# A transformer block: the first batch's softmax sums moved from TensorE to GpSimd and VectorE, loads spread over two queues, and the quantized tiles moved from GpSimd's queue to ScalarE's and SyncE's

## The chip, the core and the metric

The kernel runs on one core of a Trainium2 chip. Its engines are TensorE (PE; PEld is its loading of weights), VectorE (DVE), ScalarE (ACT), GpSimd (POOL) and SyncE (SP), which only starts transfers here. All five run their own list of instructions in order and meet at semaphores. The metric is the device time of one execution in microseconds (us), compared by medians.

## The reference

The input `x` is 4 batches of 512 rows with 512 columns. The block is an attention with 16 heads of width 32 and one shared key and value head, followed by a gated feed-forward layer with weights rounded to -1, 0 and 1; both parts end in a residual sum and a layer norm:

```python
q = rotary(heads(x @ Wq + bq)); k = rotary(x @ Wk + bk); v = x @ Wv + bv
scores = q @ k.T / sqrt(32)
ctx = softmax(scores) @ v
x = layernorm(x + ctx @ Wo + bo)
quantize(w) = clip(round(w / (mean(abs(w)) + 1e-8)), -1, 1)      # w1, w2: 1408x512, w3: 512x1408
hidden = sigmoid(x @ quantize(w1).T) * (x @ quantize(w2).T)
x = layernorm(x + hidden @ quantize(w3).T)
```

All inputs and outputs are 32-bit floats. The softmax needs, for each row and head, the sum of 512 exponentials. Where and how these sums are made in batch 0 is the heart of the change.

## The kernel before, in words

**Steps.** The main loop (L855) runs over 64 steps: 4 batches `b`, in each 4 chunks `c` of four heads, in each 4 blocks `t` of 128 key rows. I number them 0 to 63; batch 0 is steps 0 to 15. A step calls `scores` (L404): eight passes of matmuls of `kT` by `q` and eight passes that subtract the row maxima (`negm`) into two PSUM tiles `ps`, then two exponentials `es` on ScalarE. A 32-bit matmul is two passes in the trace. Then `weigh` (L445) multiplies the exponentials of the step before by `v` into `acc`, and in batch 0 `count` (L454) multiplies them by a matrix of ones into `den`: the sums. In batches 1 to 3 `den` is not used. There GpSimd adds the four blocks' exponentials into `total` (L422 to L438), and VectorE adds up over the rows afterwards.

**Maxima ahead.** In the same step `find_maxima` (L812) works 7 steps ahead (`LEAD`): matmuls `pmax` into the same two PSUM tiles that `ps` used (pool `ps_sc`, two buffers), and VectorE's maxima `mx` over them. For the steps of batch 0 this is `row_maxima` (L360), with 32-row operands; for later batches `maximum` (L371), with 128-row operands `qr` loaded from memory.

**Filling.** Between these stand pieces of other work (`fill.draw`, L763): about 1.8 us of TensorE work a step in batch 0 (`pace`, L857), which are projections `pk` and `pq` of the next batches (`project_in`, L262) with their rotations on VectorE (`turn`, L238); later also the output projection `po` and the feed-forward layer `gu`. Small chains of work (`late`) are advanced by `due` (L792), twice a step; one call is a slot.

**After a chunk.** `normalize` (L461) begins three slots after the last step of a chunk. In batch 0 it copies `den` on ScalarE, sends it to memory (`sent`), loads it back with 128 partitions (`few`), takes the reciprocal on VectorE, sends that (`flat`), and loads it with each row spread over 32 partitions (`rden`). In later batches it reduces `total` with two VectorE instructions (`part`), sends the result, loads it with 32 partitions (`few`), and reduces, inverts and transposes it before `flat`. In the end GpSimd multiplies `ctxT` by `rden` (L516).

**Quantizing.** `quantized` (L158) is a list of 66 jobs of one 128x512 tile (256 KB): 33 to find the mean of absolute values (`junk`, ScalarE), and 33 that quantize (`sgn` on ScalarE, `raw` on VectorE) and store. Jobs 0 to 20 come ahead of step 0, three after each of 7 maxima; two jobs a step follow in batch 0; the rest in batch 1. So the first weight's tiles are quantized in jobs 22 to 32 and the second's from job 44. Job k first starts the load of job k+4. Tiles of even jobs have four buffers, of odd ones five, so the load for an even job reuses the buffer of the job eight before it: if that was a quantizing one, it has to be stored first. A store is issued two jobs after its tile was quantized (L216 to L219). Loads and stores both stand in GpSimd's list (L178, L218). `sgn` is in SBUF up to step 16 and in PSUM after that (L208 to L212).

**The beginning.** SyncE issues, in this order, two small bias loads, the key and value weights, four tiles of the transposed input (`load_xT`, L121), then the query weights, `cos`, `sin` and others (L129 to L144). TensorE meanwhile does 24 matmuls of ones that nobody uses (`WARM`, L53 and L152). The first real work is `pk`, on the key and value weights and the four tiles.

**Order.** `pin` keeps each engine's instructions in the order in which the program writes them (`InOrder`, L70); `mm`, `move` and `transpose` are helpers, so most instructions carry the lines L75, L80, L83 or L86. `move` puts a transfer in SyncE's list; a wait in that list holds all later ones.

## Time and profile before

| what | value |
|---|---|
| median of 3 runs | 671.13 us (670.32 to 673.02) |
| the profiled execution | 672.56 us |
| its span, first to last instruction | 670.8 us |
| step 0 of batch 0 begins its exponentials | 49.61 us |
| step 16 (batch 1) begins its exponentials | 164.36 us |
| `den` matmuls, all in batch 0 | 128 passes, busy 16.7 us in all |
| GpSimd's adds `total`, batches 1 to 3 | 144, busy 184.3 us |
| GpSimd's issues of `raw` loads and `w` stores | 66 and 33, 0.55 us each |
| VectorE's `part`, batches 1 to 3 | 24, mean 1.23 us |

The page lists each engine's busy time and the chain of work that ended last. The chain says which instruction's end each step was waiting for; an engine's busy time does not. Groups of instructions are named out<-in by the program's tiles, followed by shapes, the count, busy time, the mean of one in ns, and the idle time ahead of them with what ended it. The timeline lists instructions in order: start, duration, engine, line, operation, tiles. Matmul ends are modelled, and matmuls that work in different rows or columns of the array overlap: eight passes of `den`, nearly 0.6 us each, take under 1 us of the chain together.

### The profile page before, as it was taken

To read this page: it belongs to the slowest core of one execution; us is meant where nothing else is said; L and a number is where in the kernel's file an instruction comes from. 1 tells how busy PE (TensorE), PEld (TensorE's weight loads), DVE (VectorE), ACT (ScalarE), POOL (GpSimd) and SP (SyncE) were. 2 spreads that over 40 slices of the span, in tenths; PEclk is the share of its full clock that TensorE was granted. 3 is DMA by queue.
4 is the path that set the end of the run, shared out by engine and by line. 5 is a ranking of instruction groups with operands and counts; after the bars stand their busy time and mean duration, and the time that the engine had idled before them with its cause. 6 is when DMAs were issued, how large, how long until landed. Compare 5 with 4: busy or idle time off the path is not lost.

```text
span 670.8 us, 9406 instructions
## 1 busy us (share of the span) xinstructions
PE 644.7 (96%) x3222; PEld 358.5 (53%) x3222; DVE 430.0 (64%) x619; ACT 282.8 (42%) x441; POOL 324.4 (48%) x414
## 2 busy tenths in 40 slices
PE   9989999999999989999999899999999999999995
PEld 6333333443333355665456466654555685778884
DVE  1896766587787867766666966676635553464335
ACT  1466555655443644333334445233435421234213
POOL 0615334535987776376666375576574802202000
PEclk9999999999999999999999999999999999999998
DMA  8755668688575286355132456351232364236531
GB/s 283 248 192 175 205 199 261 186 286 276 162 245 172 92 259 202 116 169 162 54 84 82 125 164 215 124 172 29 73 100 67 126 217 148 79 109 213 183 107 63
DMA packets 60671, 107.78 MB, mean 161 GB/s; under 512 B 14592, under 2 KB 15360, under 8 KB 60624
## 3 DMA queue, kind: packets, MB, share of 16 engines
q1 hardware_dynamic: 52560, 81.10, 38.5%
q0 software_dynamic: 7920, 25.96, 11.8%
q8 instruction: 25, 0.41, 0.3%
q14 instruction: 22, 0.18, 0.1%
q10 hardware_dynamic: 144, 0.13, 0.1%
HBM read 84.06 MB, written 23.10 MB: 160 GB/s over the span
## 4 chain that ended last, share of the span: by engine, by line
PE 81%; DVE 9%; DMA 4%; ACT 3%; issue 2%; SPq 1%; POOL 0%; DVEq 0%; ACTq 0%; POOLq 0%
PE gu L80 23%; PE po L80 19%; PE ps L80 11%; PE pmax L80 8%; PE acc L80 7%; PE pq L80 7%; DVE mx L75 3%; PE den L80 2%; DMA wg<-w 2%; ACT es L75 2%; PE pk L80 1%; DVE xt L75 1%; PE warm L80 1%; SPq L83 1%; DMA xT<-in_xT 1%
## 5 line engine op out<-in xcount | busy, mean ns | idle before, releaser
L75 DVE TENSOR_REDUCE mx<-pmax 128x1 f32<-128x512 f32 (+1 forms) x159 | 158.1, 1007 | 81.3 <-PE pmax L80 81.1
L75 ACT ACTIVATE es<-ps 128x1024 f32<-128x1024 f32 x128 | 124.2, 1022 | 141.9 <-PE ps L80 133.9
L80 PE MATMUL gu<-y,wg 128*128 128x512 f32 x704 | 172.9, 395 | 2.0 <-DMA wg<-w 1.1
L80 PEld LDWEIGHTS gu<-y,wg 128*128 128x128 f32 x704 | 131.1, 188 | 38.4 <-issue 4.7
L75 POOL TENSOR_TENSOR total<-total,es 128x512 f32<-128x512 f32 x96 | 123.8, 1319 | 45.2 <-ACT es L75 45.1
L80 PE MATMUL po<-wd,h 128*128 128x512 f32 x352 | 87.0, 395 | 4.2 <-DVE y L75 2.9
L75 POOL TENSOR_TENSOR total<-es 128x512 f32<-128x512 f32 x48 | 60.5, 1290 | 55.8 <-ACT es L75 55.8
L80 PE MATMUL pmax<-kr,qr 128*128 128x512 f32 x192 | 75.2, 455 | 3.7 <-ACT es L75 2.2
L80 PEld LDWEIGHTS po<-wd,h 128*128 128x128 f32 x352 | 64.9, 188 | 22.5 <-DVE y L75 4.6
L75 ACT CAST h<-hw 128x512 fp32r<-128x512 f32 x44 | 27.3, 620 | 100.7 <-DVE hw L75 100.7
L80 PE MATMUL acc<-es,v 128*32 128x512 f32 x512 | 68.2, 605 | 0.0
L80 PEld LDWEIGHTS pmax<-kr,qr 128*128 128x128 f32 x192 | 33.6, 188 | 57.0 <-ACT es L75 20.9
L75 DVE SCALAR_TENSOR_TENSOR hw<-th,gu 128x512 f32<-128x512 f32 x44 | 30.2, 687 | 46.9 <-PE gu L80 46.8
L80 PE MATMUL po<-wo_sb,ctxT 128*128 128x512 f32 x128 | 58.9, 593 | 0.3 <-DVE hw L75 0.3
L80 PE MATMUL ps<-negm,ones_r 2*128 2x512 f32 x256 | 58.2, 788 | 0.0
L75 DVE SCALAR_TENSOR_TENSOR xt<-po,xt 128x512 f32<-128x512 f32 x48 | 32.8, 684 | 38.1 <-PE po L80 38.1
L75 DVE TENSOR_TENSOR h<-hw,h 128x512 fp32r<-128x512 f32 x44 | 42.1, 957 | 21.7 <-ACT h L75 21.4
L80 PE MATMUL ps<-qT,kT 32*128 32x512 f32 x384 | 55.6, 640 | 0.0
L75 POOL DMA_DIRECT2D raw<-in_wf x66 | 36.1, 549 | 37.4 <-DMA w<-raw 26.7
L80 PE MATMUL pq<-xT,wq_sb 128*128 128x512 f32 x112 | 53.0, 601 | 1.0 <-ACT v L75 1.0
L75 ACT ACTIVATE th<-gu 128x512 f32<-128x512 f32 x44 | 26.3, 598 | 49.1 <-PE gu L80 49.0
L80 PEld LDWEIGHTS po<-wo_sb,ctxT 128*128 128x128 f32 x128 | 24.1, 189 | 22.0 <-issue 19.2
(98 smaller groups left out, 639.2 us busy)
## 6 DMA issues: line engine op xcount, KB each, us to landing
wg<-w SPq DMA_DIRECT2D x88, 256.0 KB
raw<-in_wf POOLq DMA_DIRECT2D x66, 256.0 KB, 4.6
qr<-qp SPq DMA_DIRECT2D x96, 128.0 KB
wd<-w SPq DMA_DIRECT2D x44, 256.0 KB
w<-raw POOLq DMA_DIRECT2D x33, 256.0 KB, 4.9
qp<-q SPq DMA_DIRECT2D x48, 128.0 KB
rden<-flat SPq DMA_DIRECT2D x64, 64.0 KB
xt<-in_x SPq DMA_DIRECT2D x16, 256.0 KB
```

Source lines behind the costliest of these rows:

```text
L75: return lambda *args, **kw: pin(getattr(self.engine, name)(*args, **kw))
L80: pin(nc.tensor.matmul(out, lhsT=lhsT, rhs=rhs, start=start, stop=stop))
L83: pin(nc.sync.dma_start(out=out, in_=in_))
```

## The change

Five edits:

1. `WARM` is 10 instead of 24. The key and value weights are loaded first; the four input tiles are issued in turn by ScalarE's queue and SyncE's; the bias loads follow in ScalarE's queue. Later calls of `load_xT` use SyncE alone, as before.
2. `count` and its matmuls are gone. The adds of `total` on GpSimd are now made in batch 0 too.
3. `normalize` takes the way of batches 1 to 3 for batch 0 (the two `part` reductions without a slot between them there), and begins four slots after the chunk instead of three in batch 0.
4. The loads of the tiles to be quantized are issued by ScalarE.
5. The stores of the quantized tiles are issued by SyncE.

```diff
-    WARM = 24
+    WARM = 10
...
-    def load_xT(n):
+    def load_xT(n, engines=(nc.sync,)):
-        for _ in range(n):
+        for k in range(n):
...
-                move(batches[b].xT[c], xT[b, :, c, :])
+                pin(engines[k % len(engines)].dma_start(out=batches[b].xT[c], in_=xT[b, :, c, :]))
...
-    move(bkv_sb, bkv)
-    move(bq_sb, bq)
     move(wkv_sb, wkv)
-    load_xT(NC)
+    load_xT(NC, (nc.scalar, nc.sync))
+    pin(nc.scalar.dma_start(out=bkv_sb, in_=bkv))
+    pin(nc.scalar.dma_start(out=bq_sb, in_=bq))
     move(wq_sb[0], wq[:, 0])
...
-                pool.dma_start(out=raws[k], in_=wf[m, f])
+                pin(nc.scalar.dma_start(out=raws[k], in_=wf[m, f]))
...
-                    pool.dma_start(out=w.bitcast(F32), in_=q)
+                    move(w.bitcast(F32), q)
...
-        if b > 0:
-            if t == 0:
-                s.first = es
+        if t == 0:
+            s.first = es
...
-    def count(b, c, t, es):
-        s = batches[b]
-        if t == 0:
-            s.den = ps_acc.tile([P, T], F32, tag="den", name="den")
-        columns(s.den, ones[:, 0:HD], es, t == 0, t == NT - 1)
...
-                if j == 0 and c + 1 < NC:
-                    yield
+            if j == 0 and b > 0 and c + 1 < NC:
+                yield
...
-            sums = work.tile([P, T], F32, tag="sums", name="sums", bufs=1)
-            act.copy(sums, s.den)
-            yield
-            sent = dram.tile([NG, T], F32, tag="flat0", name="sent", bufs=3)
-            move(sent, sums.rearrange("(i r) k -> i r k", r=HD)[:, 0])
-            yield
-            few = small.tile([P, NG * T // P], F32, tag="few", name="few")
-            move(few, sent.rearrange("i (r j) -> (i r) j", r=HD))
...
-            dve.reciprocal(few, few)
-            move(flat.rearrange("i (r j) -> (i r) j", r=HD), few)
...
-        if last is not None and last[0] == 0:
-            count(*last)
...
-            begin = slot + 3
+            begin = slot + (4 if b == 0 else 3)
```

More of the change, by code (lines that the diff above doesn't have):

```diff
@@ L421, in scores @@
             es.append(e)
-        if b > 0:
-            if t == 0:
-                s.first = es
-            elif t == 1:
-                s.total = [work.tile([P, 2, T], F32, tag=f"total{j}", name="total", bufs=1) for j in range(2)]
-                for j in range(2):
-                    for i in range(2):
-                        pool.tensor_tensor(
-                            s.total[j][:, i, :], s.first[j][:, i, :], es[j][:, i, :], ALU.add
-                        )
-            else:
-                for j in range(2):
-                    for i in range(2):
-                        pool.tensor_tensor(
-                            s.total[j][:, i, :], s.total[j][:, i, :], es[j][:, i, :], ALU.add
-                        )
+        if t == 0:
+            s.first = es
+        elif t == 1:
+            s.total = [work.tile([P, 2, T], F32, tag=f"total{j}", name="total", bufs=1) for j in range(2)]
+            for j in range(2):
+                for i in range(2):
+                    pool.tensor_tensor(
+                        s.total[j][:, i, :], s.first[j][:, i, :], es[j][:, i, :], ALU.add
+                    )
+        else:
+            for j in range(2):
+                for i in range(2):
+                    pool.tensor_tensor(
+                        s.total[j][:, i, :], s.total[j][:, i, :], es[j][:, i, :], ALU.add
+                    )
         return es
@@ L464, in normalize @@
         flat = dram.tile([NG, T], F32, tag="flat1", name="flat", bufs=3)
-        if b > 0:
-            n = T // HD
-            part = work.tile([P, NG * n], F32, tag="sums", name="part", bufs=1)
-            for j in range(2):
-                dve.tensor_reduce(
-                    part[:, ts(j, 2 * n)],
-                    s.total[j].rearrange("p i (a r) -> p (i a) r", r=HD),
-                    AX.X, ALU.add, apply_transpose=True,
-                )
-                if j == 0 and c + 1 < NC:
-                    yield
-            yield
-            parts = dram.tile([P // HD, HD, NG * n], F32, tag="parts", name="parts", bufs=3)
-            move(parts.rearrange("o r k -> (o r) k"), part)
-            yield
-            few = work.tile([HD, P // HD + 2, NG * n], F32, tag="rot_b", name="few", bufs=1)
-            move(few[:, 0 : P // HD, :], parts.rearrange("o r k -> r o k"))
-            yield
-            if c + 1 < NC:
-                yield
-            whole, lines = few[:, P // HD, :], few[:, P // HD + 1, :]
-            dve.tensor_reduce(whole, few[:, 0 : P // HD, :].rearrange("r o k -> r k o"), AX.X, ALU.add)
-            dve.reciprocal(whole, whole)
-            dve.transpose(lines, whole)
-            move(
-                flat.rearrange("(b h) (a r) -> (h a) b r", b=2, r=HD),
-                lines.rearrange("x (b r) -> x b r", b=2),
-            )
-        else:
-            sums = work.tile([P, T], F32, tag="sums", name="sums", bufs=1)
-            act.copy(sums, s.den)
-            yield
-            sent = dram.tile([NG, T], F32, tag="flat0", name="sent", bufs=3)
-            move(sent, sums.rearrange("(i r) k -> i r k", r=HD)[:, 0])
-            yield
-            few = small.tile([P, NG * T // P], F32, tag="few", name="few")
-            move(few, sent.rearrange("i (r j) -> (i r) j", r=HD))
-            yield
-            if c + 1 < NC:
-                yield
-            dve.reciprocal(few, few)
-            move(flat.rearrange("i (r j) -> (i r) j", r=HD), few)
@@ new lines, in normalize @@
+        n = T // HD
+        part = work.tile([P, NG * n], F32, tag="sums", name="part", bufs=1)
+        for j in range(2):
+            dve.tensor_reduce(
+                part[:, ts(j, 2 * n)],
+                s.total[j].rearrange("p i (a r) -> p (i a) r", r=HD),
+                AX.X, ALU.add, apply_transpose=True,
+            )
+            if j == 0 and b > 0 and c + 1 < NC:
+                yield
+        yield
+        parts = dram.tile([P // HD, HD, NG * n], F32, tag="parts", name="parts", bufs=3)
@@ new lines, in normalize @@
+        move(parts.rearrange("o r k -> (o r) k"), part)
+        yield
+        few = work.tile([HD, P // HD + 2, NG * n], F32, tag="rot_b", name="few", bufs=1)
+        move(few[:, 0 : P // HD, :], parts.rearrange("o r k -> r o k"))
+        yield
+        if c + 1 < NC:
+            yield
+        whole, lines = few[:, P // HD, :], few[:, P // HD + 1, :]
+        dve.tensor_reduce(whole, few[:, 0 : P // HD, :].rearrange("r o k -> r k o"), AX.X, ALU.add)
+        dve.reciprocal(whole, whole)
+        dve.transpose(lines, whole)
@@ L509, in normalize @@
+        move(
+            flat.rearrange("(b h) (a r) -> (h a) b r", b=2, r=HD),
+            lines.rearrange("x (b r) -> x b r", b=2),
+        )
         yield
```

## The prediction

> **What bounds the kernel now.** I read the page's first part, then the chain of waits, then the timeline of one step, then busy time step by step. Times are from the profiled execution (672.56 us, span 670.8, so 1.8 outside the span).

> ```profile
> span 670.8 us, 9406 instructions
> PE 644.7 (96%) x3222; PEld 358.5 (53%) x3222; DVE 430.0 (64%) x619; ACT 282.8 (42%) x441; POOL 324.4 (48%) x414
> ```

> TensorE looks full everywhere, so a removed matmul seems worth its whole time. The chain of one step of batch 0 seems to agree:

> ```profile
> 100.95 1.91 PE pk L80 x4
> 102.86 1.87 PE ps L80 x12
> 104.73 0.99 PE acc L80 x8
> 105.72 0.86 PE den L80 x8
> 106.58 1.09 PE pmax L80 x8
> ```

> `den`, the matmuls that the change drops, has 0.86 us of a step of 6.73. But the timeline of that step shows what stands beside it:

> ```profile
> 104.56 1.94 ACT L75 ACTIVATE es<-ps 128x1024 f32<-128x1024 f32 x2 [3.05 <-PE ps L80]
> 106.51 1.16 PE L80 MATMUL pmax<-kT,room 32*128 32x512 f32 x8
> 107.69 2.36 DVE L75 TENSOR_REDUCE mx<-pmax 128x2 f32<-128x1024 f32 x2 [4.38 <-PE pmax L80]
> 110.10 0.19 PEld L80 LDWEIGHTS ps<-room,kT 32*128 32x128 f32 x2 [0.28 <-DVE mx L75]
> ```

> The two exponentials end at 106.50, and `pmax` starts at 106.51: its two PSUM tiles are those that the exponentials empty. So `acc` and `den` fill exactly the time of the exponentials. Two reductions `mx` follow `pmax` on VectorE, and the second half of the next `ps` waits for the second of them. The loop is thus ScalarE, TensorE, VectorE in turn, with TensorE's filling inside it.

> **The change part by part.**

> 1. *The beginning: 10 warm-up matmuls for 24, the loads on two queues.* The warm-up passes alone:

> ```profile
> 1.50:4.35 2.85, 2.85 (x13) 2.85 (x14) 0.20 (x1) 1.00 0.63 143
> 4.35:7.20 2.85, 2.85 (x15) 2.85 (x14) 0.00 (x0) 1.00 0.84 206
> 7.20:9.77 2.57, 2.57 (x24) 2.54 (x22) 0.00 (x0) 1.00 1.04 352
> ```

> Twenty-eight passes in the first 5.70 us are 0.204 us each, then 24 in 2.57 are 0.107 each: TensorE doubles its pace at 7.2, though the clock column (sixth; 1.00) shows nothing. Ten matmuls are 20 passes at 0.204, so they end at 1.5 + 4.1 = 5.6 instead of 9.9. `pk` then needs its five tiles, 1.31 MB. Stretches of 2.5 us up to 7.5 and one up to 9.77 moved 2, 186, 247 and 356 GB/s: 1.09 MB by 7.5, so 1.31 at about 8.1. The two small bias loads no longer stand ahead (SP's issue of `wkv_sb` comes at 1.64 after two others; the first was at 0.73), so about 7.2, when the last quarter of `pk` is wanted. If the doubling comes at 7.2 as before, `pk` (8 passes, 3.44 us on the chain) does 1.9 passes at half pace from 5.6, and 6.1 × 0.43 = 2.6 more: it ends at 9.8 or, with a little waiting for loads, 10.0, against 13.37. **Gain 3.4.** Bounds: 1.7 (`pk` at half pace for 3.4 us more) and 4.0. From 22 to 46 us the chain is mostly VectorE's `mx` and rotations, no load, so it shifts whole. After 12 us the changed startup loads are not near the path.

> [...]

> 2. *64 `den` matmuls (128 passes) gone.* What is gained is what the loop gains, not 16 × 0.86. In steps 1 to 8, `pmax` works in row groups: its first half can start when the first exponential ends, its second only after the second, as now. Its end stays; but the first `mx` starts some 0.9 earlier, and `ps` shrinks from up to 1.87 to 1.31 (the chain's undisturbed ones). I take 6.73 to 6.3: 0.4 a step. In steps 9 to 15 `pmax` is the full-width form, whose first half moves ahead too. There the trace has the very step, in batch 1, without `den` and with one filling of 1.9:

> ```profile
> 181.26 1.94 ACT L75 ACTIVATE es<-ps 128x1024 f32<-128x1024 f32 x2 [2.83 <-PE ps L80]
> 187.04 1.02 ACT L75 ACTIVATE es<-ps 128x1024 f32<-128x1024 f32 x1 [2.74 <-PE ps L80]
> ```

> 5.78 from step to step, against 6.32 to 6.71. So TensorE's and ScalarE's part allows 8 × 0.4 + 7 × 0.64 = **7.7**. ScalarE also loses four copies of 0.62, beside other work: nothing.

> 3. *Sums to GpSimd and VectorE.* GpSimd gets 12 adds for each of four chunks at 1.3, 62 us, and loses 55 DMA issues of 0.55 in the stage; 5.2 us in three steps of four fits, and the `es` tiles (six, three steps) allow the delay. VectorE gets per chunk two `part` reductions (2 × 1.23), then 0.59 + 0.54 + 0.23 for 0.25: 3.6. That hits a VectorE whose steps alternate. The rows are steps 4, 5, 7 and 13: their length, then the busy time (and number) of PE, PEld, DVE, ACT and POOL:

> ```profile
> 76.86:83.59 6.73, 6.73 (x42) 2.22 (x40) 3.70 (x5) 4.13 (x6) 1.06 (x3) 1.00 0.75 268
> 83.59:91.18 7.59, 7.59 (x47) 2.39 (x49) 6.67 (x11) 4.05 (x7) 4.07 (x8) 1.00 0.48 142
> 97.83:104.56 6.73, 6.73 (x42) 2.22 (x40) 3.83 (x5) 3.68 (x8) 4.19 (x6) 1.00 0.62 160
> 136.88:143.59 6.71, 6.71 (x39) 2.65 (x37) 6.58 (x12) 3.95 (x7) 3.40 (x5) 1.00 0.74 235
> ```

> VectorE has 3.70, 6.67, 3.83 and 6.58 us to do. And one price is hidden: VectorE's subtraction `h<-hw,h`, two SBUF inputs, while GpSimd adds (240 to 540 us) and while GpSimd is idle (545 to 670):

> ```profile
> L75 DVE TENSOR_TENSOR h<-hw,h 128x512 fp32r<-128x512 f32 x25 | 29.0, 1160 | 9.5 <-ACT h L75 9.2
> L75 DVE TENSOR_TENSOR h<-hw,h 128x512 fp32r<-128x512 f32 x18 | 12.4, 689 | 11.5 <-ACT h L75 11.5
> ```

> 0.47 more. In batch 0 the quantizing `raw` instructions read `raw` and `sgn`, both in SBUF (from step 17 `sgn` goes to PSUM), and now run beside adds: two a step in steps 1 to 5 and 12 to 15, +0.94 a step. Taking each step as the larger of TensorE's loop and VectorE's sum: steps 1, 3, 13 and 15 become 7.0, 7.35, 7.5 and 7.25; 4 with 5 14.7; 12 (with `part`) 7.0; 14 5.8; 2, 6, 7, 8 6.3; 9 to 11 5.8. Sum 99.3 against 100.5 now. **Of 7.7 only 1.2 stays.** Ends: 7.7 (VectorE's lag absorbed by its buffers) and -3 (the contention price twice).

> [...]

> 4. *Quantized tiles: loads in ScalarE's queue, stores in SP's.* 66 issues on ScalarE; the only one there now took 0.37, SP's 0.43. From 0 (beside running ACTIVATEs) to 66 × 0.43 = 28; ScalarE idles 2 to 3.4 us ahead of most exponentials (34.7 over the stage), which hides 0.9 a step. Uncovered: the last six `junk` ahead of the first exponentials, with 0.52 of idle time: **0.4 lost**. 33 stores add two issues a step to SP, whose queue waits on others' results by then: no cost but lateness. That lateness matters: a load of job k+4 on the even buffers reuses job k-4's and must wait until its store has landed. GpSimd's queue bears it now:

> ```profile
> POOL raw L75 <- DMA w<-raw: 26.7, 6, 5.7
> ACT es L75 <- PE ps L80: 34.7, 17, 4.4
> ```

> Six waits, mean 4.45, with nothing behind them. On ScalarE `sgn` and the exponentials stand behind. But there the load comes one step (6.3) after the store, whose landing takes 5.4 in the median, so 1 to 2 remain, mostly inside the idle time: **1.0 lost** over the stage (0 to 10.5).

> 5. Batch 0's last normalization begins one slot later: the filling still has projections; 0, at most 1.

> Sum: -3.4 - 1.2 + 0.4 + 1.0 = **-3.2**, so 669.4 for an execution like the profiled one; that was 1.43 above the median 671.13, hence **667.9**.

> **Rivals.**
> - *The loop keeps its gain* (VectorE's lag absorbed, loads unheard): -3.4 - 7.7 + 0.4 = -10.7, 660.4. For it: light steps follow heavy ones; against: `mx` stands in order behind the lag. 0.22.
> - *The start gives nothing* (half pace lasts, or loads arrive no earlier): +0.2, 671.3. 0.16.
> - *ScalarE's queue is held by landings* (slower): six waits of 4.45 against 2.7 idle cost 6 × 1.75 = 10.5 instead of 1.0: +6.3, 677.4. It decides from a mean wait of about 3.4, where the loss (4.2) eats the 4.2 gained. Speaks for it: SP's stores now stand behind waits for GpSimd's `q`, later by the adds. 0.17.
> - *My forecast*, VectorE takes back the loop's gain: 665.5 to 670.5. 0.45.

> **How the numbers follow.** Range 660.4 to 674.5: it leaves out most of the slow rival. 0.5%, about what a measurement tells from no change, is 3.4 us: below 667.8 faster, above 674.5 slower. Faster 0.22 + half of 0.45 = 0.45; same 0.38; slower 0.17.

> **What would show it.** `pk` ending near 10; steps 9 to 11 near 5.8, heavy ones above 7; `raw` on VectorE near 1.2 us in batch 0 instead of 0.74; waits of ScalarE's queue for `w<-raw`, 1 to 2 us. Wrong if `raw` stays at 0.74, if the first exponentials do not come 3 us earlier, or if later batches change their steps.

## The result, and the profile after

| | before | after |
|---|---|---|
| median of 6 runs each, taken together | 672.55 us | **679.58 us** |
| lowest to highest | 670.32 to 674.25 | 678.46 to 682.12 |
| the profiled execution / its span | 672.56 / 670.8 | 682.12 / 680.3 |

The ratio is 1.0117, with a 95% interval of 1.0098 to 1.0137: slower, outside the predicted range, on the side that was given 0.17.

The first part of the page of the changed kernel, two of its rows of 40 slices, and its chain by engine; behind it the same two rows of the kernel before:

```profile
span 680.3 us, 9144 instructions
PE 641.0 (94%) x3066; PEld 353.0 (52%) x3066; DVE 452.5 (67%) x635; ACT 281.9 (41%) x437; POOL 336.3 (49%) x363
PE   8999998968999999999999899999999999999995
PEclk9998999979999999999999999999999999999998
PE 69%; DVE 14%; DMA 7%; ACT 4%; issue 3%; SPq 2%; ACTq 0%; POOL 0%; DVEq 0%; POOLq 0%
```

```profile
PE   9989999999999989999999899999999999999995
PEclk9999999999999999999999999999999999999998
```

TensorE has 156 passes less and is busy 3.7 us less, yet the span is 9.5 us longer, and its share of the chain falls from 81 to 69%. Slices 4 to 10 (51 to 170 us) are where the clock row has an 8 and a 7 and PE an 8, a 6 and an 8, which the kernel before does not have there.

The step lengths say where (from the first exponential of one step to that of the next, us; 28 and 33 are experiments told below):

| step | 0 | 3 | 5 | 8 | 9 | 12 | 13 | 15 | 16 | others of 1 to 17 |
|---|---|---|---|---|---|---|---|---|---|---|
| before | 6.39 | 6.74 | 7.59 | 6.74 | 6.51 | 6.32 | 6.70 | 6.43 | 7.91 | 61.79 |
| after | 9.64 | 7.73 | 8.39 | 9.08 | 7.47 | 11.54 | 7.67 | 9.07 | 8.66 | 58.34 |
| stores by ScalarE (e28) | 6.50 | 6.72 | 8.40 | 9.31 | 7.50 | 8.12 | 7.31 | 7.43 | 7.56 | 60.85 |
| repaired (e33) | 6.50 | 6.54 | 6.78 | 9.62 | 6.34 | 5.83 | 6.51 | 6.33 | 7.56 | 60.61 |

Step 0 begins at 46.60 us instead of 49.61: the start gained 3.0. Nine of the 18 steps give away 17.9 and the other nine win back 3.4; at step 18 the changed kernel is 11.5 behind. Steps 18 to 26 are then equal to 0.03 us each, and 1.9 come back by the end. So batch 0 and the two steps behind it hold the whole result. (In the kernel before, step 16 begins its exponentials at 156.45 us; the 164.36 of the table ahead of the prediction is where step 17 begins.)

**The start, as foreseen.** Stretches of the changed kernel: length, then busy time (and number) of PE, PEld, DVE, ACT, POOL, then the granted clock, DMA share and GB/s:

```profile
1.50:3.55 2.05, 2.05 (x9) 2.05 (x10) 0.00 (x0) 0.95 (x1) 0.15 (x3) 1.00 0.78 185
5.91:10.35 4.44, 4.44 (x10) 1.98 (x10) 0.00 (x0) 0.00 (x0) 0.00 (x0) 1.00 1.04 324
```

The warm-up still runs at 0.2 us a pass, and `pk`'s eight passes take 4.44 us and end at 10.35 (predicted 10.0; before 13.37). The second row counts ten passes because one of `warm` and one of `pq` reach into it. Two passes of `pk` run at half pace; the pace doubles at 7.6 us.

**The heaviest step, 12.** ScalarE's timeline in the changed kernel; the issue of a transfer stands as ACTq:

```profile
133.74 1.94 ACT L75 ACTIVATE es<-ps 128x1024 f32<-128x1024 f32 x2 [2.64 <-PE ps L80]
134.99 0.34 ACTq L178 DMA_DIRECT2D raw<-in_wf  x1
...
136.03 0.75 ACT L75 ACTIVATE sgn<-raw,hi 128x512 bf16<-128x512 f32 x1
144.22 0.34 ACTq L178 DMA_DIRECT2D raw<-in_wf  x1
144.66 0.72 ACT L75 ACTIVATE sgn<-raw,hi 128x512 bf16<-128x512 f32 x1 [7.88 <-DMA w<-raw]
145.28 1.92 ACT L75 ACTIVATE es<-ps 128x1024 f32<-128x1024 f32 x2
```

`sgn` has its own data long since. It stands behind the load at 144.22 in ScalarE's list, and the load waits for the landing of a store `w<-raw`, whose buffer it reuses. The exponentials stand behind both. SyncE's timeline says why the store was late:

```profile
130.28 0.31 SPq L83 DMA_DIRECT2D flat<-few  x1
130.69 1.13 SPq L83 DMA_DIRECT2D qr<-qp  x2
132.54 1.71 SPq L83 DMA_DIRECT2D rden<-flat  x4
134.29 0.42 SPq L83 DMA_DIRECT2D w<-raw  x1
134.76 0.43 SPq L83 DMA_DIRECT2D qw<-q  x1
138.49 1.75 SPq L83 DMA_DIRECT2D qp<-q  x4
140.34 1.09 SPq L83 DMA_DIRECT2D qr<-qp  x2
141.47 1.06 SPq L83 DMA_DIRECT2D w<-raw  x2
```

The store (141.47, landed 144.20) stands behind `qp`, which waited from 135.2 to 138.5 for GpSimd's `q`; and that list had just waited for the normalization's round trip (`flat` lands, which means that its transfer is complete, then `rden` may go). Before, six waits like this, 26.7 us, were in GpSimd's list with little behind them. Now there is one of 7.9 us, in the list of the exponentials.

**Step 8: a wait with no data in it.**

```profile
110.05 0.68 ACT L75 ACTIVATE kv<-pk,bkv_sb 32x512 f32<-32x512 f32 x1 [2.02 <-PE pk L80]
112.93 0.33 ACTq L178 DMA_DIRECT2D raw<-in_wf  x1
113.31 0.63 ACT L75 ACTIVATE junk<-raw 128x512 bf16<-128x512 f32 x1 [2.58 <-DMA qp<-q]
```

A load of `raw` has nothing to do with `qp<-q`. But in this trace the 619 transfers of SyncE and ScalarE take eight completion semaphores (100 to 107) between them, 77 or 78 each, and each of the 611 issues that take one again stands in its list behind a wait for that same semaphore; 85 of them take it after a transfer of the other list. The load takes 101 at 112.93, behind a wait for 101 at 112.88: SyncE's `qp<-q` of 107.72 had it last and landed at 112.85. GpSimd's 99 transfers in the trace of the kernel before have eight of their own (111 to 118).

**The clock.** After a stall TensorE is slow as well. Stretches of 3.4 us in the changed kernel (sixth number: granted clock):

```profile
45.05:48.55 3.50, 2.55 (x17) 1.11 (x16) 2.27 (x5) 2.96 (x7) 1.77 (x1) 1.00 0.53 174
48.55:51.97 3.42, 3.42 (x8) 1.34 (x7) 2.45 (x2) 1.33 (x4) 1.26 (x1) 0.50 0.29 77
51.97:55.38 3.41, 3.41 (x14) 1.31 (x16) 0.97 (x3) 0.27 (x1) 0.00 (x0) 0.50 0.00 0
...
140.70:144.10 3.40, 0.00 (x0) 0.00 (x0) 1.14 (x3) 0.00 (x0) 0.00 (x0) 1.00 0.84 271
144.10:147.50 3.40, 1.16 (x4) 0.77 (x4) 2.09 (x3) 2.54 (x3) 0.04 (x1) 0.50 0.88 252
147.50:150.95 3.45, 3.45 (x7) 1.74 (x6) 3.45 (x5) 2.01 (x4) 3.45 (x3) 0.50 0.61 173
```

### The profile page after: what moved, and what is told of

Same layout as the page of the kernel before. It is cut to its first block, busy times and chain, and to the rows that moved or that the text cites. A ratio compares the mean times of both kernels' runs of the same rounds, so it can differ in the third digit from the quotient of the medians.

```text
span 680.3 us, 9144 instructions
## 1 busy us (share of the span) xinstructions
PE 641.0 (94%) x3066; PEld 353.0 (52%) x3066; DVE 452.5 (67%) x635; ACT 281.9 (41%) x437; POOL 336.3 (49%) x363
## 4 chain that ended last, share of the span: by engine, by line
PE 69%; DVE 14%; DMA 7%; ACT 4%; issue 3%; SPq 2%; ACTq 0%; POOL 0%; DVEq 0%; POOLq 0%
PE gu L80 22%; PE po L80 17%; PE ps L80 10%; PE pmax L80 8%; PE pq L80 5%; PE acc L80 5%; DVE mx L75 5%; ACT es L75 3%; SPq L83 2%; DVE xt L75 1%; DMA qp<-q 1%; DVE part L75 1%; DMA wg<-w 1%; DMA w<-raw 1%; DVE pq L75 1%
## 5 line engine op out<-in xcount | busy, mean ns | idle before, releaser
L75 DVE TENSOR_REDUCE mx<-pmax 128x1 f32<-128x512 f32 (+1 forms) x159 | 157.8, 1005 | 65.7 <-PE pmax L80 65.5
L75 POOL TENSOR_TENSOR total<-total,es 128x512 f32<-128x512 f32 x128 | 165.5, 1325 | 52.2 <-ACT es L75 52.1
L75 ACT ACTIVATE es<-ps 128x1024 f32<-128x1024 f32 x128 | 124.1, 1021 | 146.1 <-PE ps L80 142.2
L80 PE MATMUL gu<-y,wg 128*128 128x512 f32 x704 | 172.3, 395 | 1.4 <-DVE xt L75 0.6
L80 PEld LDWEIGHTS gu<-y,wg 128*128 128x128 f32 x704 | 131.4, 188 | 36.6 <-issue 4.7
L75 POOL TENSOR_TENSOR total<-es 128x512 f32<-128x512 f32 x64 | 82.0, 1313 | 85.1 <-ACT es L75 60.9
L80 PE MATMUL pmax<-kr,qr 128*128 128x512 f32 x192 | 78.2, 466 | 14.0 <-ACT es L75 12.6
L80 PE MATMUL po<-wd,h 128*128 128x512 f32 x352 | 87.0, 395 | 4.2 <-DVE y L75 2.9
L80 PEld LDWEIGHTS po<-wd,h 128*128 128x128 f32 x352 | 65.0, 188 | 22.3 <-DVE y L75 4.5
L80 PEld LDWEIGHTS pmax<-kr,qr 128*128 128x128 f32 x192 | 34.2, 194 | 70.6 <-ACT es L75 36.1
L80 PE MATMUL acc<-es,v 128*32 128x512 f32 x512 | 69.1, 612 | 0.0
L75 ACT CAST h<-hw 128x512 fp32r<-128x512 f32 x44 | 27.3, 620 | 99.9 <-DVE hw L75 99.9
L75 DVE SCALAR_TENSOR_TENSOR hw<-th,gu 128x512 f32<-128x512 f32 x44 | 30.2, 686 | 46.5 <-PE gu L80 46.3
L80 PE MATMUL po<-wo_sb,ctxT 128*128 128x512 f32 x128 | 58.9, 593 | 0.3 <-DVE hw L75 0.3
L75 DVE SCALAR_TENSOR_TENSOR xt<-po,xt 128x512 f32<-128x512 f32 x48 | 32.8, 684 | 38.7 <-PE po L80 38.7
L80 PE MATMUL ps<-qT,kT 32*128 32x512 f32 x384 | 56.4, 640 | 2.3 <-DVE mx L75 2.3
L80 PE MATMUL pq<-xT,wq_sb 128*128 128x512 f32 x112 | 55.8, 629 | 1.0 <-ACT v L75 1.0
L75 DVE TENSOR_TENSOR h<-hw,h 128x512 fp32r<-128x512 f32 x44 | 41.8, 951 | 21.7 <-ACT h L75 21.4
L80 PE MATMUL ps<-negm,ones_r 2*128 2x512 f32 x256 | 54.7, 782 | 0.0
L75 ACT ACTIVATE th<-gu 128x512 f32<-128x512 f32 x44 | 26.3, 597 | 48.3 <-PE gu L80 48.2
L75 DVE TRANSPOSE_TENSOR_REDUCE part<-total 128x32 f32<-128x1024 f32 x32 | 38.7, 1227 | 0.0
L75 DVE SCALAR_TENSOR_TENSOR raw<-raw,hi,sgn 128x512 f32<-128x512 f32 x33 | 33.4, 1021 | 3.8 <-ACT sgn L75 3.8
```

The lines of the kernel that those rows point to most:

```text
L75: return lambda *args, **kw: pin(getattr(self.engine, name)(*args, **kw))
L80: pin(nc.tensor.matmul(out, lhsT=lhsT, rhs=rhs, start=start, stop=stop))
```

## The experiments

Each kernel was timed in rounds with the kernel before on the same chip; ratios are to that kernel, and 0.001 is 0.67 us. By the ratio the change itself cost 7.9 us.

The theories, as the expectations name them: **Q**, later **L**: ScalarE's list is held by landings of the stores whose buffers its loads reuse. **D**: without `den` TensorE has gaps of its own, and the clock falls for them. **V**: VectorE's contention with the adds. **G**, added after the first four runs: GpSimd's list is too long, and all that needs its results is late. **S**, added after `e22`: SyncE's list is the late one.

**Undoing the two transfers' edits.** `e1`: edits 4 and 5 undone.

```diff
-                pin(nc.scalar.dma_start(out=raws[k], in_=wf[m, f]))
+                pool.dma_start(out=raws[k], in_=wf[m, f])
-                    move(w.bitcast(F32), q)
+                    pool.dma_start(out=w.bitcast(F32), in_=q)
```

> The changed kernel with the quantized tiles' loads and stores back in GpSimd's list; the start and the sums stay as changed. Theory Q (ScalarE's queue is held by landings, and the held exponentials leave TensorE idle, after which its clock is halved): steps 8 and 12 lose their 2.3 and 5.2 us, so the time comes to 668 to 672; the halved windows at 117, 144 and 168 us are gone. Theory D (without den's matmuls TensorE has gaps by itself, and the clock falls for that): halved windows stay in at least two places, time 675 to 680. Theory V (VectorE beside GpSimd's adds): steps 3, 5, 9, 13 and 15 stay long, raw stays at 1.2 us, time 674 to 679 without many halved windows.

Measured: **698.16 us, 1.0377 [1.0322, 1.0432]**. All three theories fell: without edits 4 and 5 the change would have cost three times as much. GpSimd's timeline of this kernel:

```profile
80.64 0.54 POOL L75 DMA_DIRECT2D raw<-in_wf  x1
81.17 0.55 POOL L75 DMA_DIRECT2D w<-raw  x1
86.99 0.54 POOL L75 DMA_DIRECT2D raw<-in_wf  x1 [5.27 <-DMA w<-raw]
87.52 0.55 POOL L75 DMA_DIRECT2D w<-raw  x1
88.08 4.93 POOL L75 TENSOR_TENSOR total<-es 128x512 f32<-128x512 f32 x4
92.98 1.25 POOL L75 TENSOR_TENSOR q<-q,q 128x512 fp32r<-128x512 f32 x1
```

The old wait for a landing (5.27) now has the sums and `q` behind it, and so has every issue of a transfer, at 0.55 us each. With a list that holds the sums, issues these transfers and waits for their landings the kernel takes 17 us more than the changed one; what the issues and what the waits cost was not separated.

`e5`: the kernel before with edits 4 and 5 alone.

> The kernel before with edits 4 and 5 alone (loads by ScalarE's queue, stores by SyncE's). Theory Q: 676 to 682, with waits of ScalarE's list for landings of w and of 2 us and more in batch 0. Theories D and V: within 1.5 us of the kernel before (671 to 674), since den fills TensorE and GpSimd has no adds in batch 0, so q is in time, the stores are early and the loads land in time.

Measured: 673.43 us, 1.0021 [0.9994, 1.0048]. So edits 4 and 5 by themselves cost 1.4 us, with an interval from nothing to 3.2, as D and V said. But three of its ten executions took 677.4 to 679.1, the others 671.4 to 675.5. The profiled one is of the three (678.86): ScalarE waits 4.0 us for a landing of `w`, and 1.8 and 2.8 us in step 8 (9.65) for landings of SyncE's transfers `qp` and `xt`, with which its loads share only a semaphore. So the new lists can cost several us without the sums too, in some executions. The two halves of the change act on each other: the sums make the lists late, and the lists' new place puts the exponentials behind them.

`e3` and `e2` move only the stores, or only the loads, back to GpSimd (one of the two pairs of lines above each).

> The changed kernel with only the stores of the quantized tiles back in GpSimd's list; the loads stay in ScalarE's. Theory G: the stores now stand behind the sums in GpSimd's list, later than behind q in SyncE's, and ScalarE's list waits for their landing: 684 to 700. Theory L: the same sign, 680 to 690. If the stores on SyncE are what holds ScalarE's list, 672 to 677.

> The changed kernel with only the loads of the tiles back in GpSimd's list; the stores stay in SyncE's. Theory L: ScalarE's list never waits for a landing, steps 8 and 12 lose 2.5 and 5: 671 to 676. Theory G: GpSimd's list takes 0.55 for each load and the waits for landings again, its sums and q are later: 681 to 692. The kernel with both in GpSimd's list took 698.

Measured: `e3` 692.83, 1.0306 [1.0286, 1.0325]; `e2` 695.61, 1.0351 [1.0291, 1.0411]. Either half of the transfers left with GpSimd costs 13 to 16 us more than the change does; both edits are needed for the sums. Theory L's sign for `e2` was wrong; theory G had `e3`, while `e2` came out above its 681 to 692.

**The start alone.** `e4`: the kernel before with edit 1.

> The kernel before with edit 1 alone (10 warm-up matmuls, loads on two queues). All theories: step 0 begins 3.0 us earlier. If the gain is carried to the end: 669.5. If the earlier exponentials of step 0 meet a halved clock as in the changed kernel (step 0 9.6 instead of 6.4 us) without any other edit, the gain is gone: 672.5, and that loss belongs to the start and not to den. Theory D and theory Q expect 669 to 670 and no halved clock after 10 us.

Measured: 670.27 us, 0.9978 [0.9953, 1.0002]. In its profile step 0 begins 3.9 us earlier, but takes 8.02 us with one stretch of 3.4 us at the halved clock; 2.2 are left at the end. So the start can lose part of its gain with no other edit. It is not the only one that meets a halved clock in step 0: `e5`, with the old start, has 9.67 us there.

**`den` put back, unread.** `e7`:

```diff
+    def count(b, c, t, es):
+        s = batches[b]
+        if t == 0:
+            s.den = ps_acc.tile([P, T], F32, tag="den", name="den")
+        columns(s.den, ones[:, 0:HD], es, t == 0, t == NT - 1)
...
+        if last is not None and last[0] == 0:
+            count(*last)
```

> The changed kernel with the den matmuls put back, their result unused (this adds 128 passes whose output nobody reads). Theory D: they fill TensorE's gaps, no halved clock in step 0 and fewer later, time 668 to 674 in spite of the extra work. Theory Q: the waits of ScalarE's list stay (steps 8 and 12), and den costs its share of the steps again, time 677 to 684. Theory V: 677 to 684 also.

Measured: 683.09 us, 1.0171 [1.0126, 1.0217]. Theory D falls: filled with `den`, TensorE still has step 8 at 9.19 and step 12 at 11.71 us, and the halved clock after them (10.2 us of it; `e28` below, without `den`, has as much). It also gives the price of `den` in this loop: about 3.6 us (the intervals overlap), not the 16.7 of its busy time.

**One suspected delay at a time.**

```diff
# e6: the load one job later
-        AHEAD = 4
+        AHEAD = 3
# e11: sgn of batch 0 in PSUM
-                if now > PER:
+                if now >= 0:
# e18: part one step earlier
-            begin = slot + (4 if b == 0 else 3)
+            begin = slot + (2 if b == 0 else 3)
# e15: batch 0's residual input later
-        if n == NC * NT // 2:
-            late.append((slot, load_x(0)))
...
-                if b > 0:
-                    late.append((slot + 6, load_x(b)))
+                late.append((slot + 6, load_x(b)))
```

> The changed kernel with the tiles' loads issued three jobs ahead instead of four, so that a buffer is asked for half a step later after its store. Theory L (the time is lost because ScalarE's list waits for the landing of a late store): the wait of 7.9 us in step 12 shrinks by 3 us or goes, step 12 falls from 11.5 to 7 to 8.5 us, time 674 to 676. Theory G (GpSimd's list is too long: its sums wait until part has freed total, its rotations q come late, and everything behind q in SyncE's list is late): the next thing behind q is late in its place, 677 to 680. Theory V (VectorE's contention): 679 to 681.

> The changed kernel with sgn in PSUM in batch 0 too (its bank was den's), so raw has one input in SBUF only. Theory V: raw falls from 1.2 to about 0.75 us, steps 3, 5, 9, 13 and 15 lose 0.5 to 1 each, time 674 to 677. Theories G and L: raw falls as well, but the stalls of steps 8 and 12 stay; at most 1.5 us better, 678 to 680.

> The changed kernel with the normalization of batch 0 begun two slots after a chunk instead of four (part is made about one step earlier and frees total earlier). Theory G: GpSimd's waits for part (9.6 and 7.3 us) shrink to below 3, q comes up to 6 us earlier, the stores too, and steps 12 and 15 lose most of their stall: 671 to 675. Theory V: 679 to 682, since VectorE does as much as before and now waits for the last adds. Theory L expects a gain only as far as the stores come earlier: 674 to 678.

> The changed kernel with the residual input of batch 0 loaded, and its bias added by GpSimd (4 adds of 1.28 us), after the last chunk of batch 0, as in the other batches, instead of from step 8 on. Theory G: the queue of GpSimd in steps 9 to 12 (115.6 to 140 us without a gap) is 5.1 us shorter, q at 137.2 comes at about 132, step 12's stall of 5.2 shrinks to 0 to 2, time 674 to 677. Theory V: 679 to 681. If the adds merely hold GpSimd's list in batch 1 instead, 678 to 681 with longer steps 18 to 24.

Measured: `e6` 677.92, 1.0087 [1.0059, 1.0115]; `e11` 678.51, 1.0080 [1.0059, 1.0102]; `e18` 680.63, 1.0118 [1.0070, 1.0167]; `e15` 678.28, 1.0099 [1.0062, 1.0136]. No one of them repairs it. `e6` did its work in step 12 (5.83 us instead of 11.54), but steps 13, 14 and 16 took 5.4 back. `e11` brought `raw` from 1207 ns in batch 0 to 737 and gained 1.1 us by the medians, 2.5 by the ratios: contention is the smaller part. `e18` removed GpSimd's waits for `part` (16.9 us), and step 5 fell from 8.39 to 6.78, but step 8 rose to 9.87 and step 12 stayed at 12.0.

**Is GpSimd's work the cause?** `e22` leaves the key blocks 2 and 3 out of batch 0's sums.

```diff
-        else:
+        elif b > 0:
```

> The changed kernel with 16 of batch 0's 48 adds: the exponentials of the key blocks 2 and 3 are left out of batch 0's sums (32 adds of 1.3 us, 42 us of GpSimd's work, less); part and all that follows it stay. Theory G (GpSimd's list is late, with it q, the stores and the loads): steps 12 and 15 lose their stalls, only step 8's wait for another queue's landing stays (2.5): 667 to 671. Theory L without G (the landings hold ScalarE's list whatever GpSimd does, since SyncE's list is too full): 676 to 680. Theory V: raw falls to about 0.9 us, 673 to 677.

Measured: 677.96 us, 1.0085 [1.0059, 1.0111]. Theory G, which said 667 to 671, falls: with 42 us less to do, GpSimd idles before `q`, and ScalarE still waits for landings; the ratio is 2.2 us better than the change's. Its waits, then SyncE's timeline:

```profile
ACT sgn L75 <- DMA w<-raw: 8.0, 2, 5.6
ACT junk L75 <- DMA qp<-q: 2.9, 1, 2.9
```

```profile
117.19 1.06 SPq L83 DMA_DIRECT2D negm<-rows  x2
126.21 0.31 SPq L83 DMA_DIRECT2D flat<-few  x1
126.62 1.13 SPq L83 DMA_DIRECT2D qr<-qp  x2
128.51 1.71 SPq L83 DMA_DIRECT2D rden<-flat  x4
130.27 0.42 SPq L83 DMA_DIRECT2D w<-raw  x1
```

SyncE's list does nothing from 118.3 to 126.2: it waits for VectorE's `few`, and then for `flat` to land, with stores behind. The list that is late is SyncE's (theory S).

**The stores out of SyncE's list.** `e28`: the stores issued by ScalarE, all else as changed.

```diff
-                    move(w.bitcast(F32), q)
+                    pin(nc.scalar.dma_start(out=w.bitcast(F32), in_=q))
```

> The changed kernel with the stores of the quantized tiles in ScalarE's list instead of SyncE's. Theory S (SyncE's list is what is late: its in-order waits for the normalization's round trips parts, few, flat, rden and for q hold the stores behind them): step 12 falls from 11.5 to about 6.5, no wait of ScalarE for w over 2 us, time 673 to 676. Against it (ScalarE's list cannot take another 33 issues, or its stores wait for raw): 679 to 685.

Measured: **674.53 us, 1.0046 [1.0027, 1.0065]**, in the range of theory S: one line takes back 4.8 of the 7.9 us. No wait for `w<-raw` is left in ScalarE's list. Step 12 falls to 8.12 us, not to the 6.5 expected. Among what remains there are the waits with no data in them:

```profile
ACT es L75 <- DMA qp<-q: 3.2, 1, 3.2
ACT junk L75 <- DMA qp<-q: 2.8, 1, 2.8
ACT sgn L75 <- DMA qp<-q: 2.7, 1, 2.7
```

**Can the sums be kept and both kernels beaten?** `e19`: the four single edits together.

> The changed kernel with the four last edits together: normalization two slots after a chunk, loads three jobs ahead, sgn of batch 0 in PSUM, batch 0's residual input later. Each alone gave 0 to 1.7 us of 7. If G, L and V hold the loop by turns, so that taking away one leaves the next, the four together give more than their sum (about 4): 668 to 673. If they are additive: 674 to 677. If the loss has another cause: 677 to 681.

Measured: 672.67 us, 1.0010 [0.9990, 1.0031]: 7.2 us better than the change. By ratios the four alone gave 2.0, 2.5, 0 and 1.2, so whether they help each other lies within the uncertainty. In its profile step 17 begins 7.6 us ahead of the kernel before and then takes 14.2. Its chain there:

```profile
157.84 0.44 PE pmax L80
158.28 4.96 DMA xT<-in_xT
163.24 0.04 issue
163.28 3.78 PE pk L80 x4
```

Again SyncE: it issues `xT` 4.6 us after its buffer came free, because `qp`, `qr` and `parts` stand ahead. `e27` lets ScalarE issue these loads and starts batch 0's output projection at its old slot; `e30` moves the stores there as well; `e32` tries the `xT` line on the kernel before with edit 1.

```diff
-        load_xT(NC if b == 0 else 2)
+        load_xT(NC if b == 0 else 2, (nc.scalar,))
-                late.append((begin + 7, feed(b)))
+                late.append((begin + (9 if b == 0 else 7), feed(b)))
```

> The kernel with the four edits together, and two more: the projections' later xT tiles are loaded by ScalarE's queue instead of SyncE's, and the output projection of batch 0 starts at its old slot. Theory S: with the four edits step 17 began 7.6 us earlier than in the kernel before and then waited for xT, issued 4.6 us late by SyncE; with the tiles asked for in time step 17 is 8 to 9 instead of 14.2, and steps 19, 20 and 25 lose their extra 8: 662 to 667. If the wait only moves to another transfer: 669 to 673.

> The kernel before this one in this call, with the stores in ScalarE's list as well. Theory S: a little better or the same, 661 to 667, since little is behind SyncE by then. If ScalarE's list is the narrower one: 2 to 6 worse than without.

> The kernel before with edit 1 (the start) and the projections' later xT tiles loaded by ScalarE's queue. If step 17's 8.4 us of the kernel before holds a wait for xT (0.38 us seen) and little else: the same as the start alone, 669 to 671. If SyncE's list costs the kernel before as well: 666 to 669.

Measured: `e27` 673.62, 1.0012 [0.9987, 1.0037]; `e30` 680.76, 1.0136 [1.0106, 1.0166]; `e32` 670.57, 0.9971 [0.9955, 0.9987]. `e27` did repair step 17 (9.2), but its step 0 begins at 51.0, 5.5 later than in `e19`. ScalarE's timeline shows a wait without data ahead of step 0, and 3.4 us at the halved clock follow it (46.0 to 49.4):

```profile
42.65 0.34 ACTq L178 DMA_DIRECT2D raw<-in_wf  x1
43.03 0.63 ACT L75 ACTIVATE junk<-raw 128x512 bf16<-128x512 f32 x1 [3.52 <-DMA negm<-rows]
```

Four more transfers in ScalarE's list shifted which semaphore the next one takes (103, held by `negm<-rows`). `e30` is 8.3 us slower than `e27` by the ratios, above both expectations: the line that helped in `e28` hurts here, and why is not settled (its step 17 takes 14.6 us again). `e33` is `e27` with the four early loads back in SyncE's list; `e34` is the start with the same late `xT` line.

```diff
-        load_xT(NC if b == 0 else 2)
+        load_xT(*((2, (nc.scalar,)) if b else (NC,)))
```

> The kernel with four edits, batch 0's output projection at its old slot, and only the last xT tiles (those that are asked for after step 0) loaded by ScalarE's queue. In the run before, the four xT loads ahead of step 0 made ScalarE's list wait 3.5 us for a landing of negm, with which it shares no data, and step 0 came 5.5 us later. With them back in SyncE's list step 0 begins near 45.5 and steps 17, 19, 20 and 25 keep the repair: 665 to 669, the first to beat both. If the halved clock after the earlier start takes it back: 670 to 674.

> The kernel before with edit 1 and the same late xT tiles in ScalarE's queue: the start's gain alone, 669 to 671; below 668 only if step 17's wait counts without the sums too.

Measured: **`e33` 668.18 us, 0.9934 [0.9909, 0.9959]**; `e34` 670.68, 0.9969 [0.9946, 0.9992]. The first beats both kernels, by 0.7 and 1.8%. Its page:

```profile
span 666.3 us, 9150 instructions
PE 636.2 (95%) x3066; PEld 350.3 (53%) x3066; DVE 445.1 (67%) x635; ACT 282.9 (42%) x437; POOL 330.9 (50%) x363
```

Step 0 begins at 45.53, step 12 has 5.83 us. But step 8 is still at 9.62: just ahead of it ScalarE's list stands for 4.0 us, first for 1.4 and then for 1.9 us behind landings of `rden<-flat`, with which its loads (of `xT` and of `raw`) share only the semaphores 104 and 106, and then 6.8 us run at half clock. Whether the sums add to the start's own gain (2.3 us between the two) is not settled: the intervals overlap.

## Why the prediction was wrong, step by step

1. **The beginning: right, with some luck.** Predicted -3.4 at step 0; the profiled execution shows 3.0, and `e4`, `e28` and `e33` 3.9 to 4.1. `pk` ended at 10.35 (10.0), with two passes at half pace (1.9). That the pace doubled about where it did before was chance: it doubled at 7.4 us in the kernel before, at 7.6 in the changed one, at 4.7 in `e4`, at 5.3 in `e28` and `e33`, and somewhere from 4.5 to 7.6 in all profiles. The lower bound, my estimate with `pk` at half pace for 3.4 us more, did not come true in these. Not foreseen: a halved clock in step 0 that takes 1.6 (`e4`) to 3.1 us of the gain in some executions.
2. **`den`: right in kind.** Its 16.7 us of busy time were worth some 3.6 (`e7`), between the 1.2 that I kept and the 7.7 that I allowed. Of steps 9 to 11, predicted near 5.8, only step 10 ran near it, at 5.92; 9 took 7.47 and 11 took 6.29. (The steps that the prediction lists add up to 99.2, not 99.3.)
3. **VectorE: the row was right, the weight wrong.** `raw` took 1207 ns where 1.2 us was predicted: 0.47 us more in the mean than the 740 ns of the kernel before (719 to 1765 ns in single ones), and 0 more with `sgn` in PSUM (737 ns, `e11`). But taking it away gained 1.1 to 2.5 us (`e11`) for some 20 instructions at 0.47, 9.4 us of VectorE: most of it does not reach the end. That light steps absorb it was not shown by itself. GpSimd's adds, of which the prediction said "5.2 us in three steps of four fits", were at most a small cause by amount: 42 us of them less gained 2.2 (`e22`).
4. **The lists: the step that failed.** "there the load comes one step (6.3) after the store, whose landing takes 5.4 in the median, so 1 to 2 remain, mostly inside the idle time", 1.0 lost. That took the store to be issued when the program writes it. It is issued when SyncE's list gets there, and this list waited for `few`, `flat` and `q` first: 3.3 us of waiting in step 12, 7.9 in `e22`. In its place the runs show 4.8 us for the stores behind these waits (`e28`), and waits of up to 3.5 us on shared semaphores, which the prediction does not have.
5. **The slow rival** (ScalarE's queue held by landings, 677.4) had the place and the reason, SP's stores behind `q`. It was priced as six waits of 4.45; there was one of 7.9, one of 2.6 and the halved clock. It got 0.17 because the median landing was compared with the distance of two lines of the program instead of with what stands between them in SyncE's list. That its 677.4 lies near the result is therefore partly luck.
6. **The clock after a stall** had no term at all. In the profiled execution 20.5 us of the first 18 steps ran at half speed. The nearest price: step 0 of `e4`, with one such stretch of 3.4 us, takes 8.02 us, and in `e34`, without it, 6.38: 1.6 us a stretch. That part of the loss cannot be separated from the stalls that bring it on.

With the lists in better order, `e33` is 4.4 us faster than the kernel before by the ratio, near the predicted 3.2; it has further edits, so that does not confirm the sum.

Left open: how much of the remaining loss is the semaphores. Giving ScalarE's transfers semaphores of their own was not tried.

## What to carry to other kernels

Moving a wait off an idle engine is not free: before you move a transfer into another engine's list, write down what stands ahead of it there and what that waits for, then what stands behind it. A landing time says nothing about a store that has not been issued. And reckon with a slow TensorE behind a stall: in these profiles each of the 30 stretches of 3.41 us in which it was busy for less than 1.6 us, on the grid told below, was followed by a halved clock, for 3.41 us or more.

## What the runs showed of the hardware

- **Half clock after partial idleness.** In the profile of the changed kernel the clock is halved for 3.41 us or 6.83 (its very end apart), and so it is from 40 to 200 us in `e1`, `e4`, `e27`, `e28` and `e33`. The changes lie on one grid: in the changed kernel the first, where the pace doubles in the beginning, is at 7.59 us, and the others come 12, 14, 32, 33, 40, 42, 47, 48 and 196 times 3.413 us after it. The stretch ahead of a halved clock need not be idle: TensorE was busy 2.55 of 3.50 us ahead of 48.55, and 2.34 of 3.40 ahead of 168.0:

```profile
164.60:168.00 3.40, 2.34 (x12) 0.79 (x12) 3.40 (x4) 0.02 (x1) 2.11 (x2) 1.00 0.48 145
168.00:171.40 3.40, 3.40 (x13) 1.37 (x12) 0.23 (x2) 3.12 (x4) 1.28 (x1) 0.50 0.87 303
```

On that grid, which begins in each profile with its own first change, between 12 and 640 us and at full clock, the 20 profiles show this: all 30 stretches in which TensorE was busy for less than 1.6 us were followed by a halved clock, 25 of the 216 with 1.6 to 2.8 us, and none of the 3352 with more (ends of matmuls are modelled). The profiles of the kernel before and the changed one alone have 1 of 1, 3 of 18 and none of 341. What decides in the middle stays open: 2.46 us in the changed kernel (45.14 to 48.55) was followed by it, 2.45 in the kernel before (48.38 to 51.79) was not.

- **Two lists, one set of semaphores.** In these profiles ScalarE's list waited for landings of SyncE's transfers with which it shared nothing but a semaphore: 2.6 us (`qp`, step 8 of the changed kernel), 3.5 (`negm` in `e27`), and 1.4 and 1.9 in a row (`rden` in `e33`).
